# A cross-attention block with both score tiles in one group, its context two steps behind, and fixed PSUM banks

## The chip, the core and the metric

The kernel runs on one core of a Trainium2 chip. The metric is the device time of one execution in microseconds (us), the median of several runs. Five engines work beside each other and wait for each other by semaphores: TensorE (PE, with its weight loads as PEld), VectorE (DVE), ScalarE (ACT), GpSimd (POOL) and SyncE (SP), which here only issues DMAs. Each engine takes its instructions in the order in which the program lists them. PSUM, into which TensorE writes, has eight banks of 128 x 512 float32.

## What is computed

128 batches of 128 tokens with 256 channels, 16 heads of 16 channels, everything in float32:

```python
q = (query @ Wq + bq)...; k = (key @ Wk + bk)...; v = (values @ Wv + bv)...
scores = jnp.einsum('bhqd,bhkd->bhqk', q, k) / jnp.sqrt(jnp.float32(D_K))
allowed = j < i + mask                       # mask is 0: strictly earlier keys
attn = jax.nn.softmax(jnp.where(allowed, scores, NEG_INF), axis=-1)
attn = attn.at[:, :, 0, :].set(0.0)
ctx = jnp.einsum('bhqk,bhkd->bhqd', attn, v)...
x = layer_norm(query + ctx @ Wo + bo, ln1_g, ln1_b)
out = layer_norm(x + jax.nn.relu(x @ W1 + b1) @ W2 + b2, ln2_g, ln2_b)
```

Key and values are the same second input; query is x.

## The kernel before, in words

Two batches make a pair (NP = 64 pairs), and one pass of `step(p)` is a stage of a pipeline over pairs. All engines' order is the order of the calls in the source (a manual schedule), so where a call stands decides what it queues behind.

**The stations of a pair.** `tokens` (VectorE, line 241) transposes the loaded x and context blocks. `queries` and `keys` (TensorE line 256, written out by ScalarE at 267 and 278) and `values` (288, ScalarE at 298 and 303) project them. `scores(p, hi)` computes the upper 64 queries of both batches against 128 keys (hi = 1) or the lower 64 against 64 keys (hi = 0). A product there (line 322) is a tile of 32 rows by 64 columns of TensorE: strip r of four (two heads of each half m of the channels) and s, one of the two batches, which takes one half of the columns and of PSUM's partitions. `mask` (VectorE, 341) adds minus infinity and brings a score tile out of PSUM, `maximum` takes the row maximum (352) and subtracts it on POOL (353), `exponential` is ScalarE (360), `sums` adds and inverts on VectorE (372, 373) and multiplies on POOL (374). `turn` transposes the weights in blocks of 32 on VectorE (387) into `tb`, and `bring` moves the blocks across partitions by sixteen DMAs into `pT` (402). `weigh` multiplies with the values (434 and 444, tiles of 128 rows by 32 columns), `context` copies the result (ScalarE, 456), `attention_out` projects it (463). `attention_sum` (489), `stats` (476, 477), `deviation` (POOL, 483 and 484) and `norm1` (VectorE, 509; for pair 0 ScalarE, 505, after `shift` on POOL, 528) are the first norm; `residual1` (POOL, 517 and 520) prepares the second sum. `turn_x1` transposes x1 through a DRAM tile (VectorE 614, SP DMAs 233 and 236) into `x1T`; `hidden` (TensorE 647, ScalarE 653) and `second` (665) are the feed-forward part, `second_sum` (673), `scale_and_shift`, `norm2` (ScalarE, 542), `finish` (POOL, 548 and 549) and `store` the second norm. A float32 product of 128 x 128 by 256 columns shows as two TensorE records.

**Order of a step of before** on TensorE: high scores of p, `second(p - 3)`, `weigh(p - 1)`, low scores of p, queries of p + 1, `attention_out(p - 1)`, keys and values of p + 1, `hidden(p - 2)`. SP issues the loads, eight pieces of `pT` and the x1 moves; ScalarE issues the other eight pieces between its parts of `hidden`. The steps run for p = 2 to 62; pair 63 and the rest of the pipeline are written out after them, with the last pair's weights and x1 turned on TensorE (lines 417 and 222).

**PSUM before.** Score tiles lie two banks to a tile (`ps_2`, 2 buffers), everything else rotates over four banks (`ps_1`).

Of the kernel before, what the change touches and what calls it, by code (L numbers as in the profile page):

```python
# [19 lines left out]
def tile_cross_attention_block(  # L20
# [51 lines left out]
    ps_2 = ctx.enter_context(tc.tile_pool(name="ps_2", bufs=2, space=bass.MemoryType.PSUM))  # L72
    ps_1 = ctx.enter_context(tc.tile_pool(name="ps_1", bufs=4, space=bass.MemoryType.PSUM))
# [134 lines left out]

    def bank(name):
        return ps_1.tile([P, 512], F32, tag="ps1", name=name)  # L210

    def pair(name):
        return ps_2.tile([P, 2, 512], F32, tag="ps2", name=name)
# [38 lines left out]
    def project(w, src, name):  # L252
        ps = bank(name)
        for m in range(KC):
            for k in range(KC):
                nc.tensor.matmul(  # L256
                    ps[:, m * TP : (m + 1) * TP], w[:, k, m * P : (m + 1) * P], src[:, k, :],
                    start=(k == 0), stop=(k == KC - 1),
                )
        return ps  # L260

    def queries(p):
        st = states[p]
        st["qT"] = proj.tile([P, KC, TP], F32, tag="qT", name=f"qT_{p}")
        pq = project(wq, st["xT"], f"pq_{p}")
# [6 lines left out]
    def keys(p):  # L272
        st = states[p]
        st["kT"] = proj.tile([P, KC, 2, TP], F32, tag="kT", name=f"kT_{p}")
        pk = project(wk, st["cT"], f"pk_{p}")
# [7 lines left out]
    def values(p):  # L283
        st = states[p]
        pv = st["pv"] = bank(f"pv_{p}")
# [26 lines left out]
    def scores(p, hi):  # L312
# [3 lines left out]
        sps = [pair(f"pss{hi}_{p}_{t}") for t in range(2)]  # L316
        for m in range(KC):
            for s in range(2):
                first = s * P
                for r in range(NS):  # L320
                    strip = slice(32 * r, 32 * r + 32)
                    nc.tensor.matmul(  # L322
                        sps[r // 2][
                            s * HP : (s + 1) * HP, r % 2, m * 2 * n : (m + 1) * 2 * n
# [11 lines left out]
    def mask(p, hi, t):  # L336
        st = states[p]
        part = slice(t * HH, (t + 1) * HH)
        n = P if hi else HP
        no = neg.rearrange("p u j -> p (u j)") if hi else neg[:, 1, :]  # L340
        nc.vector.tensor_tensor(  # L341
            st["sm", hi][:, part, :].rearrange("p (r n) j -> p r n j", r=2),
            st["sps", hi][t][:, :, : 4 * n].rearrange("p r (n j) -> p r n j", j=n),
            no[:, None, None, :].to_broadcast([P, 2, 4, n]),
            ALU.add,
        )
# [77 lines left out]
    def weigh(p):  # L424
# [3 lines left out]
        pc = bank(f"pc_{p}")  # L428
# [29 lines left out]
    def attention_out(p):  # L458
        st = states[p]
        po = st["po"] = bank(f"po_{p}")  # L460
# [36 lines left out]
    def norm1(p):  # L497
# [4 lines left out]
        for s in range(2):  # L502
            if p == 0:

                nc.scalar.activation(
                    x1[:, s], t1[:, s], AF.Identity, bias=st["nb"][:, s], scale=sd[:, s]
# [17 lines left out]
    def shift(p, i):  # L524
        st = states[p]
        nb = st["nb"] = small.tile([P, 2, 1], F32, tag="nb", name=f"nb{i}_{p}")
# [11 lines left out]
    def norm2(p):  # L538
        st = states[p]
        t2, sd, nb = st["t2"], st["sd", 2], st["nb"]  # L540
# [98 lines left out]
    def hidden(p, fs, between=None):  # L639
        st = states[p]  # L640
        if fs[0] == 0:
            st["hT"] = ffn.tile([P, FC, TP], F32, tag="hT", name=f"hT_{p}")
        for f in fs[::2]:
            ph = bank(f"ph_{p}_{f}")
# [15 lines left out]
    def second(p, s, fs=range(FC)):  # L660
        st = states[p]
        if s == 0 and fs[0] == 0:
            st["py"] = bank(f"py_{p}")
# [80 lines left out]

    scores(0, 1)
# [8 lines left out]
    mask(0, 1, 0)  # L754
    maximum(0, 1, ONE)
    mask(0, 1, 1)
# [4 lines left out]
    mask(0, 0, 0)  # L761
    mask(0, 0, 1)
# [10 lines left out]
    mask(1, 1, 0)  # L773
# [5 lines left out]
    mask(1, 1, 1)  # L779
# [8 lines left out]
    mask(1, 0, 0)  # L788
    mask(1, 0, 1)
# [18 lines left out]
    def load_ahead(p):  # L808
        if p % 2 == 0 and p + 4 < NP:
            load([p + 4, p + 5], "x")  # L810
        if p % 2 == 1 and p + 3 < NP:
            load([p + 3, p + 4], "c")
            load_tokens((p + 3) // 2)

    def low_scores(p):
        scores(p, 0)
        mask(p, 0, 0)
        mask(p, 0, 1)
        maximum(p, 0, ALL)

    def step(p):
        nonlocal waiting
        if p > 2:
            load_ahead(p)
        scores(p, 1)
        mask(p, 1, 0)
        maximum(p, 1, ONE)
        if p > 2:
            second(p - 3, 0)
            mask(p, 1, 1)  # L830
            maximum(p, 1, TWO)
            exponential(p, 1, ONE)
            second(p - 3, 1)
            if p + 2 < NP:
                tokens(p + 2, "c")
        else:
            turn_x1_on_pe(0)
            turn_on_pe(1, 1, range(2))
            fold_norm1()
            add_b1()  # L840
            hidden(0, range(FC // 4))
            mask(p, 1, 1)
            maximum(p, 1, TWO)
            exponential(p, 1, ONE)
            low_scores(p)
            hidden(0, range(FC // 4, FC // 2))
            turn_on_pe(1, 1, range(2, 4))
            turn_on_pe(1, 0, range(2))
            hidden(0, range(FC // 2, 3 * FC // 4))
            tokens(3, "x")  # L850
            add_bo(1)
        summed = []
        sums(p, 1, ONE)
        exponential(p, 1, TWO)
        if p > 2:
            second_sum(p - 3)
            summed = [p - 3]
        else:
            tokens(3, "c")
            load_ahead(2)  # L860
            load_tokens(2)
            exponential(p, 0, ALL)
        sums(p, 1, TWO)


        weigh(p - 1)
        context(p - 1)
        if p > 2:
            scores(p, 0)
        if p == 3:  # L870
            scale_w1()
            nc.gpsimd.tensor_tensor(b1e_c, b1e_c, b1_c, ALU.add)
        queries(p + 1)
        if p > 2:
            mask(p, 0, 0)
            mask(p, 0, 1)
            maximum(p, 0, ALL)
        if p > 2:
            exponential(p, 0, ALL)
        else:  # L880
            sums(p, 0, ALL)
            add_bo(2)
        turn(p, 1, 0)
        turn(p, 1, 1)
        for q in waiting:
            finish(q)
        attention_out(p - 1)
        attention_sum(p - 1)
        if p > 2:
            sums(p, 0, ALL)  # L890
        else:
            turn(p, 0, 0)
            bring(p, nc.sync, range(NS * NS // 2))
        attention_stats(p - 1)
        if p + 2 < NP:
            tokens(p + 2, "x")
            if p == 2:
# [160 lines left out]
```

## Time and profile before

| what | value |
|---|---|
| median of 3 runs | 1586.33 us (1586.29 to 1587.1) |
| span of the profiled execution | 1585.6 us |
| instructions in the span | 41282 |
| 24.26 us of a step (808.69 to 832.95): PE busy | 24.26 us |
| the same: DVE, ACT, POOL busy | 21.67, 11.75, 20.00 us |
| last 65.5 us (from 1520.07): PE, DVE, ACT, POOL busy | 60.17, 27.68, 21.64, 33.55 us |

The profiled execution's time is its span, from the first to the last instruction; what lies around it is in the median of the runs alone. In the lines of the profile, L322 is line 322 of the kernel; a line of a group or a chain gives the engine, the line, what was written from what by the program's names, and how many instructions. The chain of waits goes back from the last instruction to what released each one. Matmul records overlap, so TensorE's busy time says that it had work, not that the array was full.

### The profile page before, as it was taken

Reading aid. Unit: us, or ns where it says so; the run is one execution under the profiler, and the core shown is the slowest. Engines: PE = TensorE matmul, PEld = TensorE weight load, DVE = VectorE, ACT = ScalarE, POOL = GpSimd, SP = SyncE. Lnnn points to the kernel's source line nnn. Section 1 sums busy time; section 2 is a strip of 40 time slices with the busy share of each in tenths; the row PEclk is TensorE's granted clock in tenths of the full one; section 3 lists DMA queues with packets and bytes.
Section 4 is the critical chain, followed back from the end, with each engine's and each line's share of the span. In section 5 each row is a group of like instructions: output and inputs, shape, how many; then the busy total and the mean of one; then the engine's idle time right before and its main releaser. Section 6 shows DMA issues by size and latency. Waiting matters only on the chain.

```text
span 1585.6 us, 41282 instructions
## 1 busy us (share of the span) xinstructions
PE 1573.8 (99%) x16514; PEld 1326.7 (84%) x16514; DVE 1370.8 (86%) x1989; ACT 757.5 (48%) x1500; POOL 1281.4 (81%) x1105
## 2 busy tenths in 40 slices
PE   9999999999999999999999999999999999999998
PEld 7788888888888888888888888888888888888887
DVE  7898988888888988898898988888889889889872
ACT  5555454444444454444444544444444455445442
POOL 7888888788787888888888888888888888888883
PEclk9999999999999999999999999999999999999999
DMA  9565665655656556556566565565555665664521
GB/s 199 115 137 128 140 147 121 150 122 130 151 127 141 138 123 157 136 123 149 127 137 148 127 149 130 117 160 128 138 134 126 152 147 121 144 137 108 127 78 34
DMA packets 479935, 210.12 MB, mean 133 GB/s; under 512 B 348672, under 2 KB 448256, under 8 KB 479744
## 3 DMA queue, kind: packets, MB, share of 16 engines
q1 hardware_dynamic: 371104, 134.29, 39.1%
q10 hardware_dynamic: 108640, 73.19, 18.0%
q8 instruction: 131, 2.15, 0.6%
q14 instruction: 60, 0.49, 0.1%
HBM read 70.00 MB, written 33.03 MB: 65 GB/s over the span
## 4 chain that ended last, share of the span: by engine, by line
PE 91%; DVE 3%; DMA 2%; POOL 1%; SPq 1%; ACT 1%; issue 1%; ACTq 0%; POOLq 0%; DVEq 0%
PE ph L647 26%; PE py L665 26%; PE pq L256 7%; PE po L463 7%; PE pk L256 6%; PE pv L288 6%; PE pss L322 6%; PE pc L444 3%; PE pc L434 2%; DMA pT<-tb 2%; SPq L402 1%; DVE su L372 1%; POOL sm L374 1%; DVE tb L387 0%; POOL sm L353 0%
## 5 line engine op out<-in xcount | busy, mean ns | idle before, releaser
L353 POOL TENSOR_TENSOR sm<-sm,nmx 128x1024 f32<-128x1024 f32 x192 | 364.2, 1898 | 118.6 <-DVE nmx L352 118.4
L647 PE MATMUL ph<-x1T,w 128*128 128x256 f32 x2048 | 453.6, 379 | 0.0
L665 PE MATMUL py<-w,hT 128*128 128x256 f32 x2016 | 453.0, 382 | 0.1
L665 PEld LDWEIGHTS py<-w,hT 128*128 128x128 f32 x2016 | 377.5, 190 | 73.4 <-issue 18.1
L374 POOL TENSOR_TENSOR sm<-sm,rs 128x1024 f32<-128x1024 f32 x192 | 364.2, 1898 | 90.1 <-DVE rs L373 84.1
L647 PEld LDWEIGHTS ph<-x1T,w 128*128 128x128 f32 x2048 | 388.7, 190 | 53.5 <-ACT x1T L632 0.5
L653 ACT ACTIVATE hT<-ph,b1e_c 128x256 f32<-128x256 f32 x504 | 208.7, 471 | 205.1 <-PE ph L647 99.2
L360 ACT ACTIVATE sm<-sm 128x1024 f32<-128x1024 f32 x192 | 201.1, 1054 | 203.9 <-POOL sm L353 195.6
L372 DVE TENSOR_REDUCE su<-sm 128x8 f32<-128x1024 f32 (+1 forms) x192 | 233.7, 1217 | 68.8 <-ACT sm L360 66.5
L341 DVE TENSOR_TENSOR sm<-pss,neg 128x1024 f32<-128x1024 f32 (+1 forms) x256 | 235.2, 940 | 51.1 <-PE pss L322 51.1
L387 DVE STREAM_TRANSPOSE tb<-sm 128x1024 f32<-128x1024 f32 x183 | 219.9, 1227 | 27.8 <-POOL sm L374 27.8
L352 DVE TENSOR_REDUCE nmx<-sm 128x8 f32<-128x1024 f32 (+1 forms) x192 | 234.3, 1220 | 6.6
L542 ACT ACTIVATE t<-t,nb,sd 128x256 f32<-128x256 f32 x124 | 67.7, 593 | 188.5 <-DMA pT<-tb 106.6
L256 PE MATMUL pq<-xT,wq 128*128 128x256 f32 x504 | 125.5, 392 | 0.0
L278 ACT ACTIVATE kT<-pk,bkh,half 128x256 f32<-128x256 f32 x252 | 120.6, 558 | 3.9 <-PE pk L256 3.8
L463 PE MATMUL po<-wo,cxT 128*128 128x256 f32 x512 | 121.1, 379 | 0.0
L288 PE MATMUL pv<-wv,cT 128*128 128x256 f32 x512 | 121.0, 379 | 0.0
L256 PE MATMUL pk<-cT,wk 128*128 128x256 f32 x504 | 119.2, 379 | 0.0
L322 PE MATMUL pss<-kT,qT 32*64 32x256 f32 (+1 forms) x4096 | 116.7, 334 | 0.0
L517 POOL TENSOR_TENSOR x1b<-x,g_r 128x512 f32<-128x512 f32 x64 | 81.5, 1273 | 34.9 <-DVE x L509 34.9
L463 PEld LDWEIGHTS po<-wo,cxT 128*128 128x128 f32 x512 | 97.2, 190 | 13.5 <-ACT cxT L456 0.3
L288 PEld LDWEIGHTS pv<-wv,cT 128*128 128x128 f32 x512 | 97.2, 190 | 13.2
(99 smaller groups left out, 1716.1 us busy)
## 6 DMA issues: line engine op xcount, KB each, us to landing
pT<-tb SPq DMA_DIRECT2D x488, 96.0 KB, 3.0
pT<-tb ACTq DMA_DIRECT2D x488, 96.0 KB, 2.7
out_dram<-t ACTq DMA_DIRECT2D x63, 256.0 KB, 2.5
xb<-in_x_dram SPq DMA_DIRECT2D x124, 128.0 KB, 4.5
cb<-in_ctx_dram SPq DMA_DIRECT2D x124, 128.0 KB, 4.3
x<-in_x_dram SPq DMA_DIRECT2D x31, 512.0 KB, 5.0
x1t<-tbx SPq DMA_DIRECT2D x248, 64.0 KB, 2.3
x1T<-x1t SPq DMA_DIRECT2D x62, 256.0 KB, 3.2
```

The costliest lines, as they stand in the source:

```text
L256: nc.tensor.matmul(ps[:, m * TP : (m + 1) * TP], w[:, k, m * P : (m + 1) * P], src[:, k, :], start=(k == 0), stop=(k == KC - 1),)
L288: nc.tensor.matmul(pv[:, s * D : (s + 1) * D], st["cT"][:, k, s * P : (s + 1) * P], wv[:, k, :], start=(k == 0), stop=(k == KC - 1),)
L322: nc.tensor.matmul(sps[r // 2][s * HP : (s + 1) * HP, r % 2, m * 2 * n : (m + 1) * 2 * n].rearrange("p (e j) -> p e j", e=2), st["qT"][str ...
L341: nc.vector.tensor_tensor(st["sm", hi][:, part, :].rearrange("p (r n) j -> p r n j", r=2), st["sps", hi][t][:, :, : 4 * n].rearrange("p r ...
L352: nc.vector.tensor_reduce(nmx[:, part], sm[:, part, :], AX.X, ALU.max, negate=True)
L353: nc.gpsimd.tensor_tensor(sm[:, part, :], sm[:, part, :], nmx[:, part, None].to_broadcast([P, part.stop - part.start, n]), ALU.add,)
L372: nc.vector.tensor_reduce(su, sm[:, part, :], AX.X, ALU.add)
L374: nc.gpsimd.tensor_tensor(sm[:, part, :], sm[:, part, :], rs[:, :, None].to_broadcast([P, part.stop - part.start, n]), ALU.mult,)
L387: nc.vector.transpose(st["tb"][:, :, at : at + 256].rearrange("p j (n a) -> p n j a", a=32), st["sm", hi].rearrange("p h j -> p (h j)")[:, ...
L463: nc.tensor.matmul(po[:, s * D : (s + 1) * D], cxT[:, k, s, :], wo[:, k, :], start=(k == 0), stop=(k == KC - 1),)
L647: nc.tensor.matmul(ph[:, i * TP : (i + 1) * TP].rearrange("p (s i a) -> p s i a", s=2, a=32), w1[:, k, (f + i) * P : (f + i + 1) * P], st[ ...
L665: nc.tensor.matmul(st["py"][:, s * D : (s + 1) * D], st["hT"][:, f, s * P : (s + 1) * P], w2[:, f, :], start=(f == 0), stop=(f == FC - 1),)
```

## The change

The pairs of banks and the rotating banks are replaced by eight named banks `b0` to `b7`, each a tile of its own. From pair 4 on, each use has a fixed bank: keys 0, values 1, queries 4, attention out 5, `second` 6, `weigh` 7; `hidden` takes 2, 3, 4, 0 in turn; high scores lie in 0 to 3, low scores of the strips 0 to 3 in 6, 7, 4, 5. `mask` is one instruction for each bank (A for strips 0 and 1, B for 2 and 3). `scores_both` issues both score tiles in one group, in blocks of two strips. In `step`, `weigh` and `context` belong to pair p - 2 (before: p - 1) and stand first, with the scores right behind; `hidden` and `second` both belong to p - 3 and stand next to each other. `norm1` runs on ScalarE (except for pair 1), with `shift` before it on POOL, between the parts of `hidden`. All sixteen `bring` DMAs of a pair are on SP. `hT` has one buffer instead of two. Pair 2 has a step of its own (`third`, the same order as before), pair 3 a shorter one (`fourth`), the steps run for p = 4 to 63, and the rest is written out anew, with the last pair's weights and x1 turned by VectorE and DMA.

```diff
-    ps_2 = ctx.enter_context(tc.tile_pool(name="ps_2", bufs=2, space=bass.MemoryType.PSUM))
-    ps_1 = ctx.enter_context(tc.tile_pool(name="ps_1", bufs=4, space=bass.MemoryType.PSUM))
+    psum = ctx.enter_context(tc.tile_pool(name="psum", bufs=1, space=bass.MemoryType.PSUM))
...
+    turns = [0]
+
+    def at_bank(i, name):
+        return psum.tile([P, 512], F32, tag=f"b{i}", name=name)
+
     def bank(name):
-        return ps_1.tile([P, 512], F32, tag="ps1", name=name)
-
-    def pair(name):
-        return ps_2.tile([P, 2, 512], F32, tag="ps2", name=name)
+        turns[0] += 1
+        return at_bank(4 + turns[0] % 4, name)
...
-        pq = project(wq, st["xT"], f"pq_{p}")
+        pq = project(wq, st["xT"], at_bank(4, f"pq_{p}") if p > 3 else bank(f"pq_{p}"))
...
-        pk = project(wk, st["cT"], f"pk_{p}")
+        pk = project(wk, st["cT"], at_bank(0, f"pk_{p}") if p > 3 else bank(f"pk_{p}"))
...
-        pv = st["pv"] = bank(f"pv_{p}")
+        pv = st["pv"] = at_bank(1, f"pv_{p}") if p > 3 else bank(f"pv_{p}")
...
-    def mask(p, hi, t):
-        st = states[p]
-        part = slice(t * HH, (t + 1) * HH)
+    def scores_both(p):
+
+        st = states[p]
+        for hi in range(2):
+            st["sps", hi] = [
+                at_bank(r if hi else (6, 7, 4, 5)[r], f"pss{hi}_{p}_{r}") for r in range(NS)
+            ]
+            st["sm", hi] = soft.tile(
+                [P, H, P if hi else HP], F32, tag=f"sm{hi}", name=f"sm{hi}_{p}", bufs=2
+            )
+            st["nmx", hi] = small.tile([P, H], F32, tag=f"nmx{hi}", name=f"nmx{hi}_{p}")
+        one, two = (0, 1), (2, 3)
+        for strips, hi, m in (
+            (two, 0, 0), (one, 1, 0), (two, 0, 1), (one, 1, 1),
+            (two, 1, 0), (two, 1, 1), (one, 0, 0), (one, 0, 1),
+        ):
+            n = P if hi else HP
+            for s in range(2):
+                for r in strips:
+                    strip, first = slice(32 * r, 32 * r + 32), s * P
+                    nc.tensor.matmul(
+                        st["sps", hi][r][
+                            s * HP : (s + 1) * HP, m * 2 * n : (m + 1) * 2 * n
+                        ].rearrange("p (e j) -> p e j", e=2),
+                        st["qT"][strip, m, first + hi * HP : first + hi * HP + HP],
+                        st["kT"][strip, m, :, first : first + n],
+                        start=True, stop=True,
+                    )
+
+    def mask(p, hi, rs):
+        st = states[p]
         n = P if hi else HP
         no = neg.rearrange("p u j -> p (u j)") if hi else neg[:, 1, :]
-        nc.vector.tensor_tensor(
-            st["sm", hi][:, part, :].rearrange("p (r n) j -> p r n j", r=2),
-            st["sps", hi][t][:, :, : 4 * n].rearrange("p r (n j) -> p r n j", j=n),
-            no[:, None, None, :].to_broadcast([P, 2, 4, n]),
-            ALU.add,
-        )
+        for r in rs:
+            nc.vector.tensor_tensor(
+                st["sm", hi][:, 4 * r : 4 * r + 4, :],
+                st["sps", hi][r][:, : 4 * n].rearrange("p (n j) -> p n j", j=n),
+                no[:, None, :].to_broadcast([P, 4, n]),
+                ALU.add,
+            )
...
-        pc = bank(f"pc_{p}")
+        pc = at_bank(7, f"pc_{p}") if p > 1 else bank(f"pc_{p}")
...
-        po = st["po"] = bank(f"po_{p}")
+        po = st["po"] = at_bank(5, f"po_{p}") if p > 1 else bank(f"po_{p}")
...
-            if p == 0:
+            if p != 1:
 
                 nc.scalar.activation(
-                    x1[:, s], t1[:, s], AF.Identity, bias=st["nb"][:, s], scale=sd[:, s]
+                    x1[:, s], t1[:, s], AF.Identity, bias=st["nb", 1][:, s], scale=sd[:, s]
                 )
...
-        nb = st["nb"] = small.tile([P, 2, 1], F32, tag="nb", name=f"nb{i}_{p}")
+        nb = st["nb", i] = small.tile([P, 2, 1], F32, tag=f"nb{i}", name=f"nb{i}_{p}")
...
-            st["hT"] = ffn.tile([P, FC, TP], F32, tag="hT", name=f"hT_{p}")
+            st["hT"] = ffn.tile([P, FC, TP], F32, tag="hT", name=f"hT_{p}", bufs=1)
         for f in fs[::2]:
-            ph = bank(f"ph_{p}_{f}")
+            if p == 0:
+                ph = bank(f"ph_{p}_{f}")
+            else:
+                ph = at_bank((2, 3, 4, 0)[f // 2], f"ph_{p}_{f}")
...
-            st["py"] = bank(f"py_{p}")
+            st["py"] = at_bank(6, f"py_{p}")
...
+        if p % 2 == 1:
+            if p + 3 < NP:
+                load([p + 3, p + 4], "c")
+            if 3 < p < NP - 1:
+                load_tokens((p + 1) // 2)
...
+    def fourth():
+        p = 3
+        load_ahead(p)
+        scores_both(p)
+        mask(p, 0, B)
+        mask(p, 1, A)
+        maximum(p, 1, ONE)
+        second(0, 0)
+        exponential(p, 1, ONE)
+        mask(p, 1, B)
+        maximum(p, 1, TWO)
+        second(0, 1)
+        scale_w1()
+        mask(p, 0, A)
+        maximum(p, 0, ALL)
+        queries(p + 1)
+        exponential(p, 1, TWO)
+        nc.gpsimd.tensor_tensor(b1e_c, b1e_c, b1_c, ALU.add)
+        sums(p, 1, ONE)
+        exponential(p, 0, ALL)
+        tokens(p + 2, "x")
+        keys(p + 1)
+        second_sum(0)
+        sums(p, 1, TWO)
+        sums(p, 0, ALL)
+        tokens(p + 2, "c")
+
+    def step(p):
+        last = p == NP - 1
+        load_ahead(p)
+        weigh(p - 2)
+        context(p - 2)
+        scores_both(p)
+        if p > 4:
+            second_sum(p - 4)
+        turn(p - 1, 1, 0)
+        if p > 4:
+            residual1(p - 3)
+            finish(p - 5)
+            add_bo(p - 1)
+        mask(p, 0, B)
+        mask(p, 1, A)
+        maximum(p, 1, ONE)
+        turn(p - 1, 1, 1)
+        if not last:
+            queries(p + 1)
+        if p > 4:
+            store(p - 5)
+        attention_out(p - 2)
+        mask(p, 1, B)
+        maximum(p, 1, TWO)
+        exponential(p, 1, ONE)
+        turn(p - 1, 0, 0)
+        bring(p - 1, nc.sync, EVERY[: 8 if last else 16])
+        mask(p, 0, A)
+        maximum(p, 0, ALL)
+        if not last:
+            keys(p + 1)
+        else:
+            bring(p - 1, nc.scalar, EVERY[8:])
+        exponential(p, 1, TWO)
+        attention_sum(p - 2)
+        values(p)
+        stats(p - 4, states[p - 4]["t2"], 2)
+        stats(p - 2, states[p - 2]["t1"], 1)
+        scale_and_shift(p - 4)
+        deviation(p - 2, 1)
+        shift(p - 2, 1)
+        values_out(p)
+        sums(p, 1, ONE)
+        exponential(p, 0, ALL)
+        sums(p, 1, TWO)
+
+        def between(f):
+            if f == 4:
+                norm1(p - 2)
+
+        hidden(p - 3, range(FC), between)
+        norm2(p - 4)
+        sums(p, 0, ALL)
+        if p + 2 < NP:
+            tokens(p + 2, "x")
+            tokens(p + 2, "c")
+        turn_x1(p - 2)
+        second(p - 3, 0)
+        second(p - 3, 1)
+
+    third()
+    fourth()
+    for p in range(4, NP):
         step(p)
 
     p = NP - 1
     weigh(p - 1)
     context(p - 1)
+    second_sum(p - 3)
+    turn(p, 1, 0)
+    turn(p, 1, 1)
+    turn(p, 0, 0)
+    bring(p, nc.sync, EVERY[:8])
+    residual1(p - 2)
     finish(p - 4)
+    add_bo(p)
     attention_out(p - 1)
     attention_sum(p - 1)
     attention_stats(p - 1)
+    shift(p - 1, 1)
+    stats(p - 3, states[p - 3]["t2"], 2)
+    scale_and_shift(p - 3)
+    bring(p, nc.scalar, EVERY[8:12])
+    store(p - 4)
+    hidden(p - 2, range(FC // 2))
+    bring(p, nc.scalar, EVERY[12:])
+    hidden(p - 2, range(FC // 2, FC))
     norm1(p - 1)
     turn_x1(p - 1)
     norm2(p - 3)
     second(p - 2, 0)
+    second(p - 2, 1)
+
     weigh(p)
     context(p)
+    second_sum(p - 2)
+    residual1(p - 1)
+    finish(p - 3)
     attention_out(p)
     attention_sum(p)
     attention_stats(p)
+    shift(p, 1)
+    stats(p - 2, states[p - 2]["t2"], 2)
+    scale_and_shift(p - 2)
+    store(p - 3)
     norm1(p)
+    turn_x1(p)
+    hidden(p - 1, range(FC))
+    norm2(p - 2)
     residual1(p)
+    finish(p - 2)
     second(p - 1, 0)
+    second(p - 1, 1)
     store(p - 2)
+
     second_sum(p - 1)
+    hidden(p, range(FC))
     stats(p - 1, states[p - 1]["t2"], 2)
     deviation(p - 1, 2)
     for s in range(2):
...
     st = states[NP - 1]
     t2 = ffn.tile([P, 2, D], F32, tag="t2", name="t2_last")
     for s in range(2):
+        py = at_bank(6 + s, f"py_last_{s}")
```

Of the part from `fourth` on, the removed lines are left out; they are in the kernel above.

## The prediction

> **What bounds the kernel now.** I read the page first: the engines' shares, the slices, the chain that ended last. Then one step in the middle, in the chain of waits.
>
> ```profile
> span 1585.6 us, 41282 instructions
> PE 1573.8 (99%) x16514; PEld 1326.7 (84%) x16514; DVE 1370.8 (86%) x1989; ACT 757.5 (48%) x1500; POOL 1281.4 (81%) x1105
> PE   9999999999999999999999999999999999999998
> PEclk9999999999999999999999999999999999999999
> PE 91%; DVE 3%; DMA 2%; POOL 1%; SPq 1%; ACT 1%; issue 1%; ACTq 0%; POOLq 0%; DVEq 0%
> ```
>
> TensorE is never free, at an undiminished clock, and is 91% of the chain. Other engines matter only where they make it wait. The chain from 800 to 826 us holds a whole step, from one low score group to the next (start, duration, what):
>
> ```profile
> 801.13 0.62 PE pss L322 x32
> 801.75 1.92 PE pq L256 x8
> 803.67 1.73 PE po L463 x8
> 805.40 1.73 PE pk L256 x8
> 807.13 1.73 PE pv L288 x8
> 808.85 6.91 PE ph L647 x32
> 815.76 1.05 PE pss L322 x32
> 816.81 7.10 PE py L665 x32
> 823.91 0.36 PE pc L434 x16
> 824.27 0.45 PE pc L444 x32
> 824.72 0.22 PE pc L434 x16
> 824.94 0.45 PE pc L444 x32
> 825.39 0.61 PE pss L322 x30
> ```
>
> The step takes 825.39 - 801.13 = 24.26 us and has no hole. The steps of pairs 3 to 62 exceed this by some 3 us in all; the clearest of those, read in the trace, are late transposed weights (pT). A gain must therefore be TensorE time. Two things in these lines decide it:
>
> - **Entry after tiled work.** 8 plain records take 1.73 us and 32 take 6.91 (0.216 each); straight after scores they take 1.92 and 7.10. The return costs 0.19 us, twice a step.
> - **Scores run in waves of eight.** The high group has 32 records of 256 columns, the low one 32 of 128: 1.05 - 0.62 = 0.43 us for 32 x 128 columns more. At 0.108 us per 128 columns of a plain record, one after the other would be 3.45: eight run at once (four row strips times two column halves). So high is 4 waves x 0.216 = 0.86, low 4 x 0.109 = 0.43, and each group pays 0.19 for filling and draining. In the first 50 ns of a high group eight records have begun, and by 0.32 us sixteen.
>
> **The change on TensorE.** Removed per step: one return to plain matmuls (0.19) and one group's fill and drain (0.19), if both tiles follow each other. If waves stayed full, the step would be 24.26 - 0.38 = 23.88.
>
> But the new order mixes sizes: strips 2 and 3 low, 0 and 1 high, the same again for the other half of the channels, then 2 and 3 high twice, then 0 and 1 low twice. Each block is only four array tiles, two records each. Reading the waves, I take records to start in program order, one waiting for its tile holding up all behind it, and the two records of a product to be laid out as now, over as many successive products as have different tiles. Starts in us of each pass, four records 0.03 apart: low(2,3) 0, high(0,1) 0.03, low 0.16 (0.05 of fill in the first pass), high 0.30; low 0.32, high 0.51, low 0.54, high 0.73; high(2,3) 0.76, 0.97; high(2,3) 1.19, low(0,1) 1.21, high 1.40, low 1.43; low(0,1) 1.54, 1.65. After the last, 0.11 of work and about 0.1 of drain: **1.86 us**, against 0.62 + 1.05 = 1.67. So 0.19 is lost where half the array idles, 0.19 is saved on one return: 24.26 + 0.19 - 0.19 = **24.26 us a step, no change**. Bounds: 1.49 with full waves (23.88), and 2.08 if products of unlike size are not laid out together, so that low and high blocks alternate four by four (24.48). I take 1.86, as now both records of all eight tiles interleave whatever the operands.
>
> The Trainium skill, "TensorE: Matmul & The Clock Gate", section "The mechanism", says matmuls are strict FIFO in start and end, no reordering; by that rule the mixed group could not reach the 23.88. The trace has no group of mixed sizes. "TensorEngine Tiling (Array Packing)", "Key Properties", says a change of tiling mode drains the engine: this speaks for the change, and by that alone the step would be the 23.88; the 0.19 of the rows is its price here.
>
> **The waits it adds.** With fixed banks, TensorE must wait for readers, and a wait there holds up every matmul behind it, so all the engines. I laid out a step from the weigh start (0): weigh to 1.48, scores 3.34, queries 5.17, attention out 6.90, keys 8.6, values 10.35, hidden 17.26, second 24.26. VectorE: TensorE to VectorE takes 0.24 us after a last product. Second sum (0.67) and one turn (1.21) end at 1.84; low scores of strips 2 and 3 come at 2.4, two masks of 256 columns (0.418 each, row L1013; no such mask is in the trace, and it lies between a 256-column statistics at 0.387 and the 512-column sum at 0.654, either of which fits) free bank 4 at 2.8 and bank 5 at 3.1 (wanted 3.34 and 5.17); high masks of 512 columns (0.654, row L489) free banks 0 and 1 by 4.3 (6.90, 8.6), banks 2 and 3 by 7.8 (10.35, 12.1); bank 6 is free at 10.5 (17.26). Context, 0.58 after 1.48, frees bank 7 at 2.3; it is wanted at 2.7. All fit; the tightest has 0.4.
>
> VectorE's busy time: two normalizations go (-2 x 0.836), four masks become eight (+0.2 high, +0.35 low): -1.1 on some 21.7. POOL gains the shift, 2 x 0.265 on 20.0, ends a step's last weighting at 23.4, and is free for the next exponents in time. ScalarE gains 2 x 0.60 (row L505) and loses eight transfers' issue; its last hT lands at 19.5, second wants it at 19.85 and 20.3. Of this I charge nothing; gone cover costs 59 us for each us of a step.
>
> SP is tighter. All sixteen pT pieces are now on its queue:
>
> ```profile
> 812.45 5.04 SPq L402 DMA_DIRECT2D pT<-tb  x8
> 818.03 2.29 SPq L233 DMA_DIRECT2D x1t<-tbx  x4
> 822.17 0.38 SPq L236 DMA_DIRECT2D x1T<-x1t  x1
> 822.59 4.15 SPq L93 DMA_DIRECT2D xb<-in_x_dram  x4
> ```
>
> 0.63 each, sixteen 10.15. The last turn ends at 10.2, the last issue begins at 19.8, and the piece lands about 3.35 after: 23.15, wanted at 24.26. x1T follows at about 28, wanted at 34.6. The load of tokens keeps two steps to its reader, so it is free; x and context loads (4.2 us) go out before the turns end. Sometimes an SP issue takes 1.1 to 2.3 us instead of 0.6; I charge 3 us for the whole run, as now.
>
> **Start and end.** To 59.5 us nothing differs. The fourth pair then has scores, second (no longer followed by a 1.35 us wait for pT), queries and keys, some 12.4 us, but the next scores need keys that ScalarE writes only after its exponents: VectorE is free at 63.4, its three maxima end at 66.6, 69.1 and 71.0, POOL's subtractions 2 us after each, ScalarE (also scaling w1, 2 x 1.14) ends the exponents at 74.9 and four keys at 76.9. So steady work begins as if at 77.0 - 1.5 = 75.5; 59 steps give 75.5 + 59 x 24.26 = 1506.9. The last step has no queries and keys, yet ScalarE, issuing eight pT pieces (0.53 each) ahead of its exponents, delays hT: it ends at 26.5. Then weigh 1.5, out 1.8, hidden 6.9, second 6.9, weigh 1.5, out 1.8, hidden and second 13.8, hidden and last second 13.8, and the present tail after TensorE of 5.5: 80.0. (All turns go by DMA, about 8 us each, beside 10 to 14 us of matmuls; the 3 us of transposes on TensorE near the end go.) Sum: 1506.9 + 80 + 3 = 1590 span. The median of the runs is 0.7 above the profiled span now (1586.33 against 1585.6), so 1590.6, rounded **1591 us**, +0.3%. Errors: 0.05 us on the score group is 3 us, start and end 4.
>
> **Rivals.**
> 1. *The mixed group runs full* (tiles take work past a waiting one): 0.37 off each of 59 steps, 1591 - 22 = **1569**, faster. For it: low and high are on different tiles and banks. Against: in the waves each start keeps program order. It decides as soon as the group is under 1.75.
> 2. *Unlike sizes are not interleaved*: 2.08 a group, 59 x 0.22 = +13: **1604**.
> 3. *pT comes late each step*: on SP from a margin of 1.1 us; with one slow issue (+1.2 us) among the sixteen in most steps plus 0.1 us of slip, 0.2 us a step, **1603**. Present slow issues mostly meet loads, which speaks against it.
>
> **Numbers.** Mine 0.45 (faster 0.03, same 0.18, slower 0.24, as the forecast stands near the bound of 0.2%, 3.2 us, which is about what a measurement can tell); first 0.20, faster; second 0.17, slower; third 0.18 (same 0.02, slower 0.16). Together 0.23, 0.20, 0.57. Own range 1583 to 1598; with the first rival's and second's ends, 1566 to 1606.
>
> **What would show it.** Scores: from first record to queries 1.86 (1.5 and 2.1 for rivals one and two). Second: 6.91, not 7.10. Queries without idle on a mask. Weigh waiting for pT: rival three. A step period of 24.26. A hole of some 3.5 us near 73. I am wrong if the period is under 24.1 or above 24.4.

## The result, and the profile after

The changed kernel takes 1601.49 us (median of 4 runs, 1598.74 to 1603.7), the kernel before 1586.71 beside it (4 runs, 1586.29 to 1588.57). The ratio is 1.0089, 95% interval 1.0075 to 1.0104: slower by 0.9%. The forecast was 1591, with 0.57 on slower. The number lies outside the forecast's own range (1583 to 1598) and inside the wide one that takes in two rivals' ends (1566 to 1606). Three of the terms behind it are wrong and partly cancel, so that it came this near is luck.

The page of the changed kernel, the lines that answer to those of before:

```profile
span 1601.9 us, 41519 instructions
PE 1565.4 (98%) x16486; PEld 1355.3 (85%) x16486; DVE 1272.8 (79%) x2125; ACT 794.6 (50%) x1616; POOL 1304.0 (81%) x1229
PE   8799999999999999999999999999999999999988
PEclk9899999999999999999999999999999999999999
PE 87%; DVE 4%; DMA 3%; SPq 2%; issue 1%; POOL 1%; ACT 1%; ACTq 0%; POOLq 0%; DVEq 0%
```

TensorE is now less than full in the first two and the last two slices, the clock drops in the second, and the chain has lost 4% of PE, by these lines one each to VectorE, DMA and SP's issuing (SPq). The middle still looks full. Its steps are faster than before, as the chain of waits shows for 800 to 826 us (start, duration, what; the chain goes through 44 of the group's 64 records):

```profile
808.86 6.91 PE py L698 x32
...
816.80 0.45 PE pc L474 x32
817.25 1.55 PE pss L357 x44
818.80 1.92 PE pq L257 x8
820.72 1.73 PE po L493 x8
```

One score group of **1.55 us** stands where 0.62 and 1.05 stood, second takes 6.91 and no longer 7.10, only the queries still pay the 0.19. From one such step to the next it is 23.94 us (23.944 in the median), not 24.26. Over 58 steps that is 18 us of gain, and yet the run is 16 us longer. Where the time is, against the forecast's own sum (the start of weigh in step 5 and in step 63 are read from the score groups at 115.00 and 1517.42, less 1.48 for weigh):

| part | forecast | profile | difference |
|---|---|---|---|
| start, to weigh of step 5 | 99.8 | 113.5 | +13.7 |
| 58 steps, undisturbed | 58 x 24.26 = 1407.1 | 58 x 23.944 = 1388.8 | -18.3 |
| what these steps take beyond that | 3.0 | 13.6 | +10.6 |
| last step and the rest | 80.0 | 86.0 | +6.0 |
| span | 1589.9 | 1601.9 | +12.0 |

**Start.** The chain of waits of the changed kernel around the fourth pair's second:

```profile
66.05 1.85 DVE sm L371 x4
...
71.58 0.34 DVE sm L371
71.92 0.04 issue
71.97 10.12 PE py L698 x32
```

The scores of pair 3 are done by 63.7. TensorE then stands for 8.2 us until VectorE has masked low strip 0, its last mask but one, because second(0) accumulates in bank 6 and that strip lies in bank 6. Behind the hole second is slow: 10.12 us and not 6.91. The view by stretches says why (stretch, its length, busy time and count of PE, PEld, DVE, ACT, POOL, then the granted clock, DMA share, GB/s):

```profile
72.00:77.00 5.00, 5.00 (x12) 4.01 (x13) 3.37 (x5) 2.34 (x3) 4.92 (x4) 0.50 0.72 130
```

In these 5 us after the hole the granted clock is 0.50: 12 records where 23 would fit. VectorE waits 6.8 us for second, whose sum stands at the head of its queue.

The 13.7 us of the first row are 2.7 of the first 60 us (the scores of pair 3 begin at 62.17, not 59.5), 7.3 of this hole and its slow records (see e1_start), and 3.7 behind them, nearly all in these: weigh and scores of step 4 take 1.5 us more than usual, 1.0 of it in two waits for kT, and weigh of step 5 takes 2.05 us more, as it waits for pT.

**Last step.** ScalarE has eight pieces of pT to issue ahead of its exponents, and they wait for VectorE's turn:

```profile
1526.48 0.29 ACTq L432
...
1529.20 3.42 DMA pT<-tb
...
1536.32 0.37 ACT hT L686
1536.69 0.04 issue
1536.73 9.90 PE py L698 x32
```

Hidden's products end at 1530.0, its last activation at 1536.7: a hole of 6.7 us, and second again takes 9.90 instead of 6.91.

**Holes in the score group.** Ten of the 57 groups from step 6 to step 62 take more than 1.55 us: 20, 21, 24, 45 to 48, 50, 51 and 54, by 9.3 us in all. The chain around that of step 54:

```profile
1299.82 0.58 PE pss L357 x10
1300.40 1.32 issue
1301.72 1.30 PE pss L357 x33
```

"issue" means that nothing the profile shows was waited for: no bank, no operand. What the trace does show is a transfer of 16,384 bytes on the instruction queue, from 1298.83 to 1300.39; each of the larger holes has one that ends 1.2 to 1.5 us before TensorE goes on. There are 131 of them for TensorE's 2 x 16486 matmuls and weight loads and 640 waits, so one brings 256 instructions. That the holes are instructions which came late is read from this; e3_shift, e8_pad and e9_pad_early test it. A step has 512 matmuls and weight loads and 10 waits of their own, 522 in all: the boundary of a block moves by 10 a step and meets the same place again after 25.6 steps, as 20 to 24 and 45 to 50 do.

### The profile page after: what moved, and what is told of

It is laid out like the page before. It is cut to its first block, busy times and chain, and to the rows that moved or that the text cites. A ratio compares the mean times of both kernels' runs of the same rounds, so it can differ in the third digit from the quotient of the medians.

```text
span 1601.9 us, 41519 instructions
## 1 busy us (share of the span) xinstructions
PE 1565.4 (98%) x16486; PEld 1355.3 (85%) x16486; DVE 1272.8 (79%) x2125; ACT 794.6 (50%) x1616; POOL 1304.0 (81%) x1229
## 4 chain that ended last, share of the span: by engine, by line
PE 87%; DVE 4%; DMA 3%; SPq 2%; issue 1%; POOL 1%; ACT 1%; ACTq 0%; POOLq 0%; DVEq 0%
PE py L698 25%; PE ph L680 24%; PE pq L257 7%; PE po L493 6%; PE pk L257 6%; PE pv L289 6%; PE pss L357 6%; PE pc L474 3%; PE pc L464 2%; SPq L432 2%; DVE sm L371 2%; DMA vd<-vz 1%; DVE nmx L382 1%; DVE tb L417 1%; POOL sm L383 1%
## 5 line engine op out<-in xcount | busy, mean ns | idle before, releaser
L698 PEld LDWEIGHTS py<-w,hT 128*128 128x128 f32 x2016 | 386.9, 192 | 68.6 <-DVE sm L371 8.2
L404 POOL TENSOR_TENSOR sm<-sm,rs 128x1024 f32<-128x1024 f32 x192 | 359.2, 1898 | 11.8 <-DVE rs L403 11.7
L371 DVE TENSOR_TENSOR sm<-pss,neg 128x512 f32<-128x512 f32 (+1 forms) x512 | 250.6, 539 | 23.9 <-PE pss L357 20.3
L706 DVE TENSOR_TENSOR t<-py,x1b 128x512 f32<-128x512 f32 x63 | 43.6, 692 | 240.2 <-issue 180.4
L402 DVE TENSOR_REDUCE su<-sm 128x8 f32<-128x1024 f32 (+1 forms) x192 | 225.7, 1175 | 7.9 <-ACT sm L390 7.9
L417 DVE STREAM_TRANSPOSE tb<-sm 128x1024 f32<-128x1024 f32 x186 | 229.2, 1234 | 1.7 <-DMA x1t<-tbx 1.4
L486 ACT COPY cxT<-pc 128x508 f32<-128x508 f32 x64 | 37.3, 583 | 347.0 <-PE pc L474 347.0
L686 ACT ACTIVATE hT<-ph,b1e_c 128x256 f32<-128x256 f32 x504 | 195.4, 471 | 17.4 <-PE ph L680 17.3
L268 ACT ACTIVATE qT<-pq,bqs_c 128x256 f32<-128x256 f32 x126 | 52.8, 470 | 190.2 <-PE pq L257 190.2
L357 PE MATMUL pss<-kT,qT 32*64 32x256 f32 (+1 forms) x3904 | 103.3, 330 | 6.5 <-issue 5.3
```

What stands on the lines that cost most here:

```text
L371: nc.vector.tensor_tensor(st["sm", hi][:, 4 * r : 4 * r + 4, :], st["sps", hi][r][:, : 4 * n].rearrange("p (n j) -> p n j", j=n), no[:, No ...
L402: nc.vector.tensor_reduce(su, sm[:, part, :], AX.X, ALU.add)
L404: nc.gpsimd.tensor_tensor(sm[:, part, :], sm[:, part, :], rs[:, :, None].to_broadcast([P, part.stop - part.start, n]), ALU.mult,)
L417: nc.vector.transpose(st["tb"][:, :, at : at + 256].rearrange("p j (n a) -> p n j a", a=32), st["sm", hi].rearrange("p h j -> p (h j)")[:, ...
L698: nc.tensor.matmul(st["py"][:, s * D : (s + 1) * D], st["hT"][:, f, s * P : (s + 1) * P], w2[:, f, :], start=(f == 0), stop=(f == FC - 1),)
```

## The experiments

My theories, before the runs: the steps gain because the passes of the mixed group start as their own tile comes free; the loss is the wait for bank 6 in the fourth pair, ScalarE's eight issues in the last step, and late instructions in the dense stretch of weigh and scores (some 330 instructions in 3 us). Rivals: VectorE's work sets the start anyway, something else sets the last step, the holes are bank waits or loads.

**e1_start: the fourth pair masks bank 6 first**

```
 def fourth():
...
     scores_both(p)
-    mask(p, 0, B)
+    mask(p, 0, A)
...
-    mask(p, 0, A)
+    mask(p, 0, B)
     maximum(p, 0, ALL)
```

> Edit: in the fourth pair alone, the mask of low strips 0 and 1 changes places with that of low strips 2 and 3, so that the bank which second(0) takes over (bank 6, low strip 0) is masked first and not last. Theory: the 8.2 us hole of TensorE from 63.73 to 71.97 was the wait for that mask alone, and the 16 records at 427 ns after it (3.2 us) came from the hole. VectorE starts its masks at 66.05, so second(0) starts near 66.5, 5.5 us earlier, and ends 7 to 9 us earlier; steps 5 and on come earlier by that, and the median is 1592 to 1595 against 1601.5. Rival: VectorE's own work up to the turned pieces of pair 3 sets the next step anyway (weigh of pair 3 waits longer for pT), so that under 3 us are saved: 1599 or more.

Measured: 1592.79 us (5 runs), 1.0034 of before (1.0021 to 1.0047), **8.7 us** less than the changed kernel. In its profile the scores of pair 3 begin at 60.45 (62.17 in the changed kernel's, see p1_before below), second 4.3 us behind them (9.8) and takes 8.9 (10.1); from these scores to those of step 5 it is 45.5 us (52.8). So the order of the masks costs 7.3 us. TensorE still waits 2.4 us there, as VectorE begins its masks only at 64.3. The two profiles differ by 12.3 us: beside the 7.3 there are 1.7 up to the scores of pair 3 and 3.9 in the 58 steps, and both of these vary between profiles of kernels that share this code. The theory holds.

**e2_end: no issues by ScalarE in the last step**

```
-    bring(p - 1, nc.sync, EVERY[: 8 if last else 16])
+    bring(p - 1, nc.sync, EVERY)
...
-    else:
-        bring(p - 1, nc.scalar, EVERY[8:])
```

> Edit: in the last step all 16 pieces of pT are issued by SP, as in the steps before, and none by ScalarE ahead of its exponents. Theory: the 6.7 us hole of TensorE from 1530.01 to 1536.73 ahead of second(60), and the records at 427 and 588 ns after it, came from those 8 issues; without them second(60) starts within 0.5 us of the end of hidden, the last step ends 24 to 25 us after its start (30.6 in the changed kernel), and the median is 5 to 8 us lower, 1594 to 1597. Rival: the exponents of the last step come late for another reason, or weigh of pair 62 then waits for its pieces on SP, and less than 2 us are saved: 1599 or more.

Measured: 1594.56 us (4 runs), 1.0042 of before (1.0025 to 1.0059), **6.9 us** less. From its weigh to the end of second the last step takes 23.3 us (1513.29 to 1536.61; 30.6 in the changed kernel), less than forecast. Second still waits 1.2 us for hT, more than the 0.5 that I gave. The theory holds.

**e3_shift: 128 instructions ahead of everything**

```
+    for i in range(32):
+        nc.tensor.matmul(warm[:32, 0:32], ident[:32, :32], ident[:32, :32], start=True, stop=True)
     states[0] = {}
```

> Edit: 32 more small products (32x32) after the warming transposes at the very start, which put every later instruction of TensorE 128 places further on; 128 is half of the 256 instructions that one 16,384 byte transfer of the instruction queue brings. Nothing else changes. Theory: the holes inside the score group (steps 20, 21, 24, 45 to 48, 50 and 54 in the changed kernel, 0.4 to 1.9 us each) come where a transfer of instructions falls into weigh and the scores; a step moves the place by 10 instructions of 256, so 128 places are 12.8 steps. The holes of steps 20 to 24 are gone and others stand near steps 7 to 11, 32 to 41 and 58 to 62; the sum of the holes stays between 5 and 20 us, and the time within 10 us of 1601.5. Rival: the holes are waits for a bank, or a clash with the loads, and stay at the same steps.

Measured: 1609.27 us (one run; its start is 4.4 us later). The steps whose score group takes over 0.1 us more than usual, with the excess in us:

```
changed  20 1.42, 21 1.89, 24 0.92, 45 0.66, 46 0.90, 47 0.41, 48 0.61, 50 0.70, 51 0.13, 54 1.65
shifted   7 1.39,  8 0.96, 10 0.69, 12 0.63, 32 0.55, 33 2.74, 34 2.09, 36 0.47, 38 1.45,
         58 0.84, 59 1.79, 60 0.29
```

The pattern moved by 13 steps, as computed from 128 / 10, and nothing is left at the old steps. In the largest, of step 33, the chain of waits has 2.14 us of "issue". Loads and banks did not move against the steps, so they are out as the cause.

**e4_far: the blocks of the score group in an order that strict starts would punish**

```
-    (two, 0, 0), (one, 1, 0), (two, 0, 1), (one, 1, 1),
-    (two, 1, 0), (two, 1, 1), (one, 0, 0), (one, 0, 1),
+    (one, 1, 0), (one, 1, 1), (two, 1, 0), (two, 1, 1),
+    (one, 0, 0), (one, 0, 1), (two, 0, 0), (two, 0, 1),
```

> Edit: the eight blocks of the score group are issued in another order, high of strips 0 and 1 twice, high of strips 2 and 3 twice, then low of strips 0 and 1 twice, low of strips 2 and 3 twice; the records, tiles and banks are the same. Theory that the group's passes start as their own tile comes free, also past a record that waits in front of them: each tile has the same work, 4 high and 4 low passes, so the group stays between 1.55 and 1.8 us. Rival, the forecast's step: records start strictly in the program's order, so that strips 2 and 3 stand idle while the first blocks run; high of strips 0 and 1 starts its last pass at 0.79, high of strips 2 and 3 at 1.58, low of strips 0 and 1 at 1.97, and the group takes about 2.5 us. In between, a limited look ahead gives 1.8 to 2.3. Period: 23.94 plus what the group takes over 1.55.

Measured: 1641.59 us (one run), period 24.75. A group and the queries after it, from the trace of this kernel (start, busy, then the idle time before it and its cause):

```profile
435.52 1.85 PE L357 MATMUL pss<-kT,qT 32*64 32x256 f32 x64
437.87 1.99 PE L257 MATMUL pq<-xT,wq 128*128 128x256 f32 x8 [0.50 <-DVE sm L371]
```

A group of the changed kernel in the same view:

```profile
817.18 1.62 PE L357 MATMUL pss<-kT,qT 32*64 32x128 f32 x64
```

The busy time goes to the end of the last record, so 1.85 compares with 1.62 here, and not with 1.55, which ends where the queries start. The far order costs 0.23 us; by the measure of 1.55 that makes some 1.78, inside what I gave the theory and far from the 2.5 of strict order. The 32 high records start in four rounds of eight, 0.22 to 0.27 apart, although in the order of the calls sixteen records of strips 0 and 1, on four tiles, stand ahead of the first of strips 2 and 3. In the low half the first two rounds and the last two have four each: six rounds of 0.11 and not four, which is the 0.23 us. So records pass others that wait, over at least this distance, but not without limit; the limit I did not measure. Most of the rest of the 0.8 us by which the period rises is a bank (0.50 idle): low strips 2 and 3 now come last, are masked first, and hold bank 4 against the queries. This is the wait that the forecast priced and that the change's own order avoids.

**e5_both: the edits of e1_start and e2_end together**

> Edit: the two edits of e1_start and e2_end together, nothing else of the changed kernel undone. Theory: the losses at the start (8.7 us) and in the last step (6.9 us) lie one after the other on the path and add, so that the median is 1601.5 - 15.6 = 1586, within 2 us; against 1586.9 of the kernel before that is no difference, because the holes in the score group (some 13 to 16 us) still eat what 59 steps of 0.32 us give. Rival: the two overlap, or the earlier start moves the holes, and the time is 1589 or more.

Measured: 1586.29 us (11 runs), 0.9995 of before (0.9986 to 1.0004). The two gains add (8.7 + 6.9 = 15.6; 15.2 measured). With start and end mended the change is even with the kernel before.

**e6_between: queries between weigh and scores (on e5_both)**

```
     weigh(p - 2)
     context(p - 2)
+    if not last:
+        queries(p + 1)
     scores_both(p)
...
-    at_bank(r if hi else (6, 7, 4, 5)[r], ...)
+    at_bank(r if hi else (5, 6, 4, 7)[r], ...)
```

Strips 0 and 1 change places with 2 and 3 in the order of the low masks and of the blocks; the queries after the scores go.

> Edit: e5_both, and the queries of the next pair are put between weigh and the score group, so that the 200 instructions of weigh and the 128 of the scores no longer follow each other; strips 0 and 1 change places with 2 and 3 in the order of the blocks and of the masks, and the banks of the low tile become 5, 6, 4, 7, so that no bank is waited for. Theory that the holes are late instructions: with 1.7 us of plain passes in the middle, no idle of 0.4 us or more is left inside the score group in any step from 6 on (nine such steps in the changed kernel), and a step without a hole costs 0.1 to 0.4 us more than 23.94 for one more return to plain passes; 59 steps of that cost 6 to 24 us, the holes give back 13 to 16, so the median is within 12 us of e5_both. Rival, that the holes have another cause that is tied to the scores' own tiles or banks: they stay, and the time is e5_both plus 6 to 24 us.

Measured: 1661.44 us (4 runs), 1.047 of before (1.0456 to 1.0484). No group from step 6 to step 62 takes over 1.60 us, at whatever place the block boundary stands: the holes are gone, which speaks for late instructions, though this run cannot tell the plain passes in between from the new waits that follow. But the period is 25.35, 1.4 us more, far over my 0.1 to 0.4. The waits of TensorE (us, times, longest) say why:

```profile
PE py L698 <- ACT hT L686: 38.6, 120, 1.2
```

Scores 1.7 us later make masks, maxima, exponents and so hT later, and second waits for hT twice in every step. I had costed the move on TensorE only and left out the chain through VectorE, POOL and ScalarE. As a mend it fails; the time says nothing about the holes.

**e7_norm: the first norm back on VectorE**

```
-    if p != 1:
+    if p == 0:
         nc.scalar.activation(x1[:, s], t1[:, s], ...)
```

> Edit: the changed kernel with one part undone, the first norm back on VectorE for every pair but the first (two instructions of about 1.3 us a step); start and end are as in the changed kernel. VectorE is busy 79% of the span, 18.9 us of a 23.94 us step, and would be at 21.5. If this part of the change carries the shorter step, the period rises: the turned pieces of pT, which SP sends with about 1 us to spare before weigh, come up to 2.6 us later, weigh waits for them, and the period is 24.3 to 25.5, the time 1620 to 1690. If VectorE's 5 us of idle time take it in, the period stays within 0.05 of 23.94 and the time within 5 us of 1601.5.

This kernel, against what its expectation says, has the edits of e1_start and e2_end in it too, so it is compared with e5_both. Measured: 1620.74 us (4 runs), **34.4 us** over e5_both; between the two profiles it is 37.4, of which 31.0 lie in the 58 steps and some 5 of these in more holes in the score group (12.0 in place of 6.9). VectorE is busy 93% of the span. TensorE's waits:

```profile
PE pc L464 <- DMA pT<-tb: 20.8, 18, 2.3
```

Nearly every second step is 0.5 to 2.2 us longer, and most others stay at 23.94. SP's rows of a long one and of the next, a usual one (start, duration of the sixteen issues):

```profile
804.58 12.91 SPq L432 DMA_DIRECT2D pT<-tb  x16
```

```profile
829.40 11.42 SPq L432 DMA_DIRECT2D pT<-tb  x16
```

In the long one the chain of waits puts the last nine issues behind the transfer of vd, which ScalarE issues behind exponents that wait for POOL:

```profile
807.88 3.99 DMA vd<-vz
811.87 0.02 issue
811.89 0.51 SPq L432
```

In the usual one the last of the sixteen issues begins at 840.25, 0.6 us before the row ends. With the median of 2.2 us from the start of an issue to its landing (this profile's own) its piece is there at 842.4, and weigh begins at 843.05: 0.6 us of slack, so a turn or an issue that is later by more shows at once. Without the norm on ScalarE the shorter step is not kept in half of the steps; the other parts of the change were not undone one by one. Why only every second step is long, I did not settle.

**e8_pad and e9_pad_early: jumps in the instruction count (on e5_both)**

```
     turn_x1(p - 2)
+    if p in (19, 36, 53):        # e9_pad_early: (13, 30, 47)
+        pt = at_bank(7, f"pad_{p}")
+        for i in range(20):
+            j = i % NS
+            nc.tensor.matmul(pt[32 * j : 32 * j + 32, :32], ident[:, :32], ident[:, :32],
+                             start=True, stop=True)
     second(p - 3, 0)
```

> Edit: e5_both, and in steps 19, 36 and 53 alone 20 small products (32 columns of the identity into columns of bank 7 that nothing reads) ahead of second, which puts all later instructions of TensorE 80 places further on each time. Theory that the holes depend on where a block of 256 instructions begins: counted from step 20, the place moves by 10 a step, holes were at 0 to 60 and at 250 to 256, and the three jumps step over that stretch (80 at step 20, back to 80 at step 37 and to 80 or so at step 54). No hole of 0.4 us or more is left in the score group from step 6 on; the holes and the slow records behind them, 10 to 13 us in e5_both, go, the pads cost at most 1 us each, and the median is 1573 to 1579 against 1586.3. Rival, that the holes follow the steps or the loads: they stay and the time is 1586 to 1589.

> Edit: the same three pads as e8_pad, in steps 13, 30 and 47, so that each jump lands in the bad stretch instead of passing over it. Theory: holes stand in steps 14 to 19, 31 to 36 and 48 to 53 (three stretches where e5_both has two), none in 20 to 25 or 39 to 46, and the time is 1588 to 1597. Rival: that the pads help for another reason, or not at all, makes it the same as e8_pad.

Measured: e8_pad **1581.49 us** (6 runs), 0.9968 of before (0.9955 to 0.9980): 0.3% faster than the kernel before. e9_pad_early, the same work in other steps, 1588.87 us (10 runs), 1.0010 (1.0001 to 1.0019). A pad takes 0.49 us, and 0.2 for the changes of tiling. Excess of the score groups:

```
e5_both        20 1.13, 21 1.62, 24 0.94, 45 0.57, 46 0.72, 48 0.98, 50 0.93
e8_pad         54 0.49
e9_pad_early   17 0.73, 18 0.95, 20 1.24, 31 0.97, 48 1.45, 50 0.49, 52 1.48
```

The holes go where the jump passes over the bad stretch and appear where it lands in it. One of 0.49 us, in step 54, is left where I had said none would be. Among TensorE's waits from 125 to 1500 us e9_pad_early has this line, and e8_pad has none for the scores:

```profile
PE pss L357 <- issue: 3.6, 5, 1.1
```

The gain of e8_pad is 4.8 us, less than the 7 to 13 that I expected: I had counted what all steps take beyond 23.94 in e5_both (10.3 us), of which only 6.9 are these holes; the pads cost 2.0; and stops of 0.3 to 0.8 us in weigh at some even steps remain (22, 24, 38, 42, 56, 60); among TensorE's waits in the same window, those in weigh are 1.1 us of "issue" in two and 0.9 us for a DMA in three, and I did not look for the cause further. In e9_pad_early the stretches are as expected but for step 20, one step past the first.

**p1_before and p2_before: the kernel before, profiled twice more**

> The kernel before, unchanged, profiled once more, to see how much its first 60 us vary by themselves. Scores of pair 3 begin at 59.5 in its profile and at 60.3 to 63.3 in ten profiles of kernels that share the changed kernel's first 60 us; there the transposes after the hole at 23 to 27 us run at a granted clock of 1.00 or of 0.55 to 0.68. If the clock after that hole is a matter of the moment, the kernel before also shows a later start, 60 to 62.5, and a clock under 1 in some profile; if the changed start costs the time, it shows 59.3 to 59.7 again.

> The same as p1_before, a second look at the same: either 59.3 to 59.7 and a clock of 1.00 again, or up to 62.5 with a clock under 1 between 25 and 30 us.

Measured: scores of pair 3 begin at 60.04 and 60.06 (59.51 in the first profile) with a clock of 1.00 from 25 to 30 us, which is neither of the two things that I had named. The 24 transposes around that time take 4.74 us in all three, from the first to the scores behind them. In the kernels with the changed start these take 5.6 us where the clock is 1.00 (e1_start, e5_both, e6_between, e8_pad), 6.36 at 0.92 (e7_norm) and 7.0 to 7.3 at 0.55 to 0.68 (the changed kernel, e2_end, e4_far, e9_pad_early). So the changed start costs 0.9 us by itself, and 0.8 to 1.7 more in those profiles where the clock is down behind a hole of TensorE. The hole is one of 2.65 us there, where the kernel before has two of 0.76; why it is so was not tried. What lies ahead of the transposes varies as well: they begin at 22.7 to 25.2 us in kernels with the same start, so that e6_between, at a clock of 1.00, comes to the scores of pair 3 at 63.0.

## Why the prediction was right and wrong

- **The steady step, "no change": wrong.** The step that failed is "I take records to start in program order, one waiting for its tile holding up all behind it", which gave 1.86 us a group. Measured 1.55: in the trace of step 6 the first pass of the second low block starts (139.83) before the second pass of the high block (139.85), which stands ahead of it in the order of the calls. By the forecast's own sign, wrong if the period is under 24.1, this step failed. With 1.55 for 1.67 and one return of 0.19 less the step should fall by 0.31; it fell by 0.32. The first rival, given 0.20, had the mechanism; its 1.49 and 23.89 are 0.06 and 0.05 off. The rule that I set beside it, strict order of starts (the Trainium skill, "TensorE: Matmul & The Clock Gate", "The mechanism"), does not hold for records on different tiles in these traces, as 1.55 against 1.86 and, in e4_far, 1.85 against 2.5 show.
- **The bank waits of a step: right.** In the whole run the queries and hidden wait for a mask once each, 0.5 us, both outside the steady steps. VectorE has 19.84 us of work in the step from 817.18, where the forecast's sum gives some 20.6.
- **The start: wrong, the largest error (13.7 us).** The forecast worked out that bank 6 comes free last, at 10.5, and is wanted at 17.3; for the fourth pair it then laid scores and second end to end, "12.4 us", without asking the same question, though there second follows the scores directly. e1_start prices this at 7.3 us. The hole that the forecast did expect, 3.5 us near 73 for the keys, came to two waits of 0.5 us. That "to 59.5 us nothing differs" was wrong too, by 2.7 us in this profile, and weigh of step 5 waits 2.05 us for pT, which the start's sum did not hold.
- **The last step: right in kind, too small.** "ScalarE, issuing eight pT pieces ahead of its exponents, delays hT" is what happened; it ended 30.6 us after its start and not 26.5. Left out: ScalarE also waits for VectorE's turn before it can issue, and second runs at half clock behind the hole. e2_end prices it at 6.9 us.
- **SP: tighter than forecast in the step shown.** Sixteen issues take 11.54 us there, not 10.15:

```profile
802.03 11.54 SPq L432 DMA_DIRECT2D pT<-tb  x16
```

  The last one begins at 812.98, 21.2 us after the start of the step's weigh and not 19.8. Its piece lands 2.2 us later and not 3.35, at 815.2, and the next weigh begins at 815.7: the margin is 0.5 us, not 1.1. Of the 13.6 us that the steps take beyond 23.94 some 4 are late pT and slow records; 3 were charged.
- **Not foreseen:** holes from late instructions, 9.3 us in the score groups of the changed kernel, with slow records behind the longest. The trace of before held as many transfers of the instruction queue (131) and no hole; its longest such stretch, weigh and the low scores, has some 260 instructions in 2.1 us, no less dense than here (330 in 3.0) but shorter. That the length makes the difference was not tried by itself. The Trainium skill, "Runtime: NRT & Kernel Launch", "Instruction fetch mechanics", says that the crossing of a block is mostly hidden; here up to 2.1 us of it is not (e3_shift, step 33).

The forecast's leaning to slower, 0.57, was right for other reasons than its own: the result's sign came from start and end, not from the rivals that I had named for slower (unlike sizes not interleaved; pT late in each step); neither is in these traces. What stays open: how far TensorE looks past waiting records, the 0.9 us of the first 60, the stops in weigh, and why every second step of e7_norm is long.

## What to carry to other kernels

When a resource is reassigned, ask who takes it over next in every phase, the first and last rounds too: the steady step was safe by 7 us in the forecast, the fourth pair lost 7.3 to the very same bank. A long hole of TensorE costs more than its length, as the work behind it starts at half clock. And once the records of a stretch become short and many, count instructions as well as microseconds: here two tiled groups side by side ran TensorE dry of them in some ten steps.

## What the hardware showed that I had not expected

- Small products on different array tiles start out of program order: 1.55 us for a mixed group that strict order, by the forecast's count, would run in 1.86.
- 256 instructions are one transfer; two tiled groups in a row (some 330 instructions in 3 us) stop TensorE for 0.4 to 2.1 us, not in every step, when a block boundary falls in a stretch of 60 to 90 of the 256 places, differing from run to run. Jumping over it with 80 small instructions costs 0.7 us each time; three jumps left one hole of 0.49 us where there had been seven.
- The granted clock is 0.50 in the 5 us behind a hole of 8.2 us, and the stretch from 25 to 30 us of kernels with the same start runs at 0.55 to 1.00 in different profiles.
